# Cross-attention over 64 sequences: weights loaded in whole chunks, and two biases spread on the chip

## The chip, the cores and the metric

The kernel runs on one core of one Trainium2 chip. The metric is the device time of one execution in microseconds. Before the change the median of three runs is 1337.42 us (1336.81 to 1337.81).

## The reference

Everything is fp32. For each of 64 batch entries there are 256 text rows x of width 512 and 256 audio rows c of width 384. The constants of the shapes are B = 64, L = S = 256, H = 512.

```python
text_p = einsum('bld,dh->blh', x, W_text) + b_text
audio_p = einsum('bsd,dh->bsh', c, W_audio) + b_audio
Q = layer_norm(text_p, g1, beta1)
K = layer_norm(audio_p, g2, beta2)
alpha = softmax(einsum('blh,bsh->bls', Q, K) / sqrt(512))
H_hyper = einsum('bls,bsh->blh', alpha, audio_p)
H_hyper = einsum('blh,hk->blk', H_hyper, W_out) + b_out
out = layer_norm(H_hyper + x, g_out, beta_out)
```

## The kernel before, in words

The five engines are TensorE (PE), VectorE (DVE), ScalarE (ACT), GpSimd (POOL) and SyncE (SP). The whole program is one list of calls in the file. Each call (`k[0].multiply(0, [0])`, `q2.six()`) issues one or a few instructions on its engine, and each engine works through its own in the order of the list; semaphores hold an instruction until its inputs are there. So the list is the schedule. It has an opening, a loop over the batch entries 3 to 60 in which five entries are in work at different stages, and an ending. The products of the loop are split by recursive schemes with fewer multiplies (`Fork` for the queries, `Thirds` for the keys and for the output), whose sums of operands stand on DVE and POOL.

The opening is where the change is. Batch entry 0 has no transposed input yet: `RowTurn` takes its rows (c_0, x_0), puts their columns in the kernel's order on DVE (`arrange`), transposes them on PE (tile ps_rows) and copies them to SBUF on ACT (cT, xT). `Projection.multiply(t, chunks)` then multiplies 128 rows by chunks of 128 rows of the weight, 512 wide, into a PSUM bank: ps_m and ps_l for the keys of entry 0, ps_u and ps_n for its queries, ps_f for the keys of entry 1. `evict` adds the bias, so it needs the bias in all 128 partitions. `means` and `centre` take the mean of each weight row and of the bias away. `turn_weights` transposes w_audio (ps_wa), and `fold_multiply` multiplies it by w_out. At the very start `keep_busy(6)` lets PE multiply a tile of ones that nobody reads.

Rows of a weight are dealt to partitions so that partition 32q + i of chunk k holds row 32(qK + k) + i, with q from 0 to 3 and K chunks (3 for w_audio, 4 for w_text). In DRAM a chunk is therefore four separate blocks of 32 rows of 2 KB.

SP issues nearly all DMA requests, in its own order. Eight semaphores are used in turn, so a request also waits until the one eight places before it has landed; ACT issues two requests at the start. `squares` loads an entry in four requests of 32 partitions.

Of the kernel before, what the change touches and what calls it, by code (L numbers as in the profile page):

```python
# [22 lines left out]
def kernel(  # L23
# [87 lines left out]
    nc.gpsimd.memset(ones, 1.0)  # L111
# [16 lines left out]

    x_0 = xin.tile([P, LT, D], F32, tag="x", name="x_0")
# [59 lines left out]
    class RowTurn:  # L189
# [6 lines left out]

        def tile(self, t):
            ar = self.ar[:, t]
            arrange(ar, self.rows[:, t, :], self.chunks, nc.vector.tensor_copy)
            ps = p_at.tile([P, self.chunks, P], F32, tag="at", name="ps_rows")  # L200
            for j in range(self.chunks):
                nc.tensor.transpose(ps[:, j, :], ar[:, j, :], ident)
            nc.scalar.copy(self.T[:, :, bass.ts(t, P)], ps)
# [1195 lines left out]

    keep_busy(6)  # L1400
    war = []
    bt_row = bt_sb.rearrange('p (o h) -> p o h', o=1)
    c_turn = RowTurn(c_0, AC, 'cT')
    var_0 = small.tile([P, 4], F32, tag='var4', name='var')
    wa_t = const.tile([P, 11, WP], F32, tag='wa_thirds', name='wa_thirds')
    wao_room = const.tile([P, HC * H], F32, tag='wo', name='wao_thirds')
    pool, tag = (once, 'e')
    c_turn.tile(0)
    k[0] = Projection('k', 0, c_turn.T, wa_sb, ba_sb, AC, ST, bank[0:2])
    war.append(pool.tile([P, HC, P], F32, tag=tag, name=f'war_{0}'))  # L1410
    x_turn = RowTurn(x_0, DC, 'xT')
    c_turn.tile(1)
    k[0].multiply(0, [0])
    pool, tag = (work, 'eT')
    k[0].multiply(1, [0])
    arrange(war[0], wa_sb[:, 0, :], HC, nc.gpsimd.tensor_copy)
    q[0] = Projection('q', 0, x_turn.T, wt_sb, bt_sb, DC, LT, bank[2:4])
    war.append(pool.tile([P, HC, P], F32, tag=tag, name=f'war_{1}'))
    arrange(war[1], wa_sb[:, 1, :], HC, nc.gpsimd.tensor_copy)
    k[0].multiply(1, [1])  # L1420
    mean_wa = means(wa_sb, AC, 'mwa')
    pool, tag = (work, 'eT')
    war.append(pool.tile([P, HC, P], F32, tag=tag, name=f'war_{2}'))
    k[0].multiply(0, [1])
    k[0].multiply(1, [2])
    arrange(war[2], wa_sb[:, 2, :], HC, nc.gpsimd.tensor_copy)
    x_turn.tile(0)
    ba_row = ba_sb.rearrange('p (o h) -> p o h', o=1)
    x_turn.tile(1)
    k[0].multiply(0, [2])  # L1430
    turn_weights(0, 1)
    q[0].multiply(1, [0])
    q[0].multiply(1, [1])
    centre(wa_sb, mean_wa, AC)
    mean_wt = means(wt_sb, DC, 'mwt')
    mean_ba = means(ba_row, 1, 'mba')
    q[0].multiply(0, [0])
    k[0].evict(1)
    k[0].evict(0)
    third_weights(wa_sb, wa_t, [0])  # L1440
    k[0].scales()
    k[0].normalise([1])
    q[0].multiply(0, [1])
    bt_step = const.tile([P, H2], F32, tag='bt_step', name='bt_step')
    mean_bt = means(bt_row, 1, 'mbt')
    cT[1] = turn_c(1)
    k[0].normalise([0])
    q[0].multiply(0, [2])
    q[0].multiply(0, [3])
    turn_weights(1, 1)  # L1450
    turn_weights(2, 1)
    k[1] = Projection('k', 1, cT.pop(1), wa_sb, ba_sb, AC, ST, bank[4:6])
    q[0].multiply(1, [2])
    k[1].multiply(1, [0])
    centre(ba_row, mean_ba, 1)
    k[1].multiply(0, [0])
    turn_weights(3, 1)
    k[1].multiply(1, [1])
    third_weights(wa_sb, wa_t, [2], nc.vector)
    xT[1] = turn_x(1)  # L1460
    q[0].multiply(1, [3])
    k[1].multiply(1, [2])
    k[1].multiply(0, [1])
    k[1].multiply(0, [2])
    fold_multiply(1, 0, 1)
    xs_1 = SumX(xT.pop(1), nc.vector)
    centre(wt_sb, mean_wt, DC)
    centre(bt_row, mean_bt, 1)
    q[0].evict(1)
    g1_sb, be1_sb, g2_sb, be2_sb, bac_sb = take_columns()  # L1470
    wa_blocks = third_weights(wa_sb, wa_t, [3])
    q[0].evict(0)
    wt_blocks = weight_sums(wt_sb, DC // 2, 'wtsum')
    fold_multiply(1, 1, 2)
    k[0].store()
    xs_1.add(1)
    xs_1.add(1)
    load_c(2)
    folds.append(p_at.tile([P, H], F32, tag='at', name='ps_fold'))
    xs[1] = xs_1  # L1480
    k[1].evict(1)
    q[1] = Fork(1, xs.pop(1).of, wt_blocks)
    load_x(2)
    k[1].evict(0)
    xs_1.add(1)
    fold_multiply(1, 2, 3)
    q[0].scales()
    fold_multiply(0, 0, 1)
    third_weights(wa_sb, wa_t, [1], nc.vector)
    part = bias_parts()  # L1490
    load_c(3)
    cT[2] = turn_c(2)
    Fork.seed()
    cs[2] = Sides(cT.pop(2), 'csum')
    q[0].normalise([0])
    cs[2].add(1)
    fold_multiply(2, 0, 1)
    q[1].seven()
    cs[2].add(1)
    cs[2].add(1)  # L1500
    q[1].one()
    nc.vector.tensor_tensor(bt_step, bt_sb[:, :H2], bt_sb[:, H2:], ALU.subtract)
    nc.vector.tensor_scalar(g2_sb, g2_sb, scale, None, ALU.mult)
    q[1].after_seven()
    xT[2] = turn_x(2)
    k[0].fetch()
    q[0].normalise([1])
    nc.vector.tensor_scalar(be2_sb, be2_sb, scale, None, ALU.mult)
    xs[2] = SumX(xT.pop(2))
    xs_1.add(1)  # L1510
    q[0].store()
    fold_multiply(0, 1, 2)
    fold_multiply(0, 2, 3)
    q[1].after_one()
    k[1].square()
    k[1].scales()
    q[1].six()
    q[1].start_q3()
    fold_multiply(0, 3, 4)
    q[1].step_r()  # L1520
    fold_evict(0)
    cs[2].add(1)
    cs[2].add(1)
    cs[2].add(1)
    load_x(3)
    Thirds.seed_with(ba_sb)
    cT[3] = turn_c(3)
    xs[2].add(1)
    cs[2].add(1)
    load_c(4)  # L1530
    bias_rest(part, 1, 2)
    fold_multiply(1, 3, 4)
    xs[2].add(1)
    ba_delta = third_bias(ba_sb, 'ba_delta')
    cs[3] = Sides(cT.pop(3), 'csum')
    k2_0 = k[2] = Thirds('k', 2, cs.pop(2), wa_blocks, ba_sb, ba_delta)
    q[0].fetch()
    q[1].five()
    k2_0.one()
    fold_evict(1)  # L1540
    q[1].after_five()
    xs[2].add(1)
    at_0 = att[0] = Attention(0)
    xs[2].add(1)
    cs[3].add(1)
    k2_0.copy_n1()
    q[2] = Fork(2, xs.pop(2).of, wt_blocks)
    k[1].normalise([0])
    k2_0.two()
    k[1].normalise([1])  # L1550
    at_0.k.turn()
    cs[3].add(1)
    q[1].two()
    third_weights(wa_sb, wa_t, [4], nc.vector)
    q[1].three()
    k2_0.start_t()
    cs[3].add(1)
    q[1].four()
    xT[3] = turn_x(3)
    q[1].square()  # L1560
    k[1].store()
    q[1].scales()
    fold_multiply(2, 1, 2)
    k2_0.three()
    k2_0.copy_t()
    var_2 = small.tile([P, 4], F32, tag='var4', name='var')
    fold_multiply(2, 2, 3)
    q2_0 = q[2]
    k2_0.start_l0()
    k2_0.start_l1()  # L1570
    cs[3].add(1)
    q[1].normalise([0])
    q[1].normalise([1])
    bias_rest(part, 2, 3)
    fold_multiply(2, 3, 4)
    q[1].store()
    cs[3].add(1)
    k2_0.four()
    Fork.seed()
    xs[3] = SumX(xT.pop(3))  # L1580
    cs[3].add(1)
    at_0.affine_keys(0)
    q2_0.one()
    k2_0.take_m()
    bias_rest(part, 3, 4)
    k2_0.start_u()
    q2_0.seven()
    q2_0.after_one()
    xs[3].add(1)
    fold_evict(2)  # L1590
    at_0.affine_keys(3)
    at_0.q.turn()
    load_c_rows(1)
    q2_0.six()
    q2_0.after_seven()
    q2_0.start_q3()
    load_x(4)
    k2_0.five()
    at_0.affine_queries(3)
    xs[3].add(1)  # L1600
    at_0.affine_queries(0)
    q[1].fetch()
    cs[3].add(1)
    k2_1 = k[3] = Thirds('k', 3, cs.pop(3), wa_blocks, ba_sb, ba_delta)
    last_1 = att[0]
    xs[3].add(1)
    k2_0.copy_n()
    k2_0.copy_u()
    xs[3].add(1)
    q[3] = Fork(3, xs.pop(3).of, wt_blocks)  # L1610
    q2_0.step_r()
    q2_0.five()
    k2_0.leave_middle()
    wao_t = wao_room[:, :11 * WP].rearrange('p (n h) -> p n h', n=11)
    at_0.affine_keys(2)
    at_0.affine_keys(1)
    k2_0.middle_d()
    k2_0.leave()
    q2_0.after_five()
    q2_1 = q[3]  # L1620
    fold_bias(part)
    k2_0.square(var_0[:, 2:], [0])
    at_0.score(0, 1)
    k2_0.leave_ends()
    at_0.affine_queries(2)
    q2_0.three()
    at_0.affine_queries(1)
    k2_0.middle_sum()
    k2_0.square(var_0[:, 2:], [1])
    third_weights(wao_sb, wao_t, [1])  # L1630
    q2_0.two()
    k2_0.seed()
    k[1].fetch()
    q2_0.four()
    at_0.score(1, 2)
    load_c(5)
# [289 lines left out]
    for b in range(3, B - 3):  # L1926
# [32 lines left out]
        if b + 4 < B: load_c(b + 4)  # L1959
# [516 lines left out]
```

## Time and profile before

| what | value |
| --- | --- |
| median of three runs | 1337.42 us |
| the profiled execution's own time | 1338.2 us |
| its span, first to last instruction | 1336.0 us |
| granted TensorE clock | 1.000 |
| instructions | 29959 |
| mean traffic of the DMA engines | 241 GB/s |

The profiled execution's own time includes 2.2 us that lie outside the span. In the rows that follow, a line such as `13.23 1.72 PE ps_n L440 x4` of the chain of waits means that from 13.23 us on, for 1.72 us, four records of PE that write the tile ps_n from line 440 were what the end waited for. An fp32 multiply leaves two records. The matmul rows' ends are modelled, and a few records can be missing. The DMA rows give the requests by tile, their size, and the median time from the issue to the landing where the profile can tell it.

### The profile page before, as it was taken

What the parts mean: (1) busy time and instruction counts of PE and PEld (TensorE: products, weight loads), DVE (VectorE), ACT (ScalarE), POOL (GpSimd) and SP (SyncE); (2) the same over time, 40 slices, a digit from 0 to 9 for tenths busy, and PEclk for the clock granted to TensorE, in tenths of its full rate; (3) what the DMA queues carried; (4) which work ended last, traced back from release to release, by engine and by line L of the source; (5) the groups of instructions that cost most, each with busy time, mean ns of one, the idle gap of its engine ahead of it and who ended that gap; (6) DMA issues with size and microseconds to landing.
All of it is one profiled execution on the core that took longest, in us unless ns stands there. A gap on an engine that the chain in (4) does not pass through costs nothing.

```text
span 1336.0 us, 29959 instructions
## 1 busy us (share of the span) xinstructions
PE 1328.3 (99%) x8495; PEld 1249.6 (94%) x8495; DVE 1243.0 (93%) x3313; ACT 1162.9 (87%) x3310; POOL 1151.5 (86%) x1855
## 2 busy tenths in 40 slices
PE   9999999999999999999999999999999999999998
PEld 5899999999999999999999999999999999999996
DVE  6769999999999999999999999999999999999968
ACT  4898898898898898988988988988889889889885
POOL 5798898898898898988988988988989889889865
PEclk9999999999999999999999999999999999999999
DMA  9988989888888889889888898889988998888773
GB/s 220 243 235 236 242 246 246 242 255 240 251 251 247 245 247 240 259 244 238 255 234 242 253 243 247 243 230 266 254 235 251 255 240 252 246 244 253 209 229 138
DMA packets 448971, 322.24 MB, mean 241 GB/s; under 512 B 153765, under 2 KB 381349, under 8 KB 448806
## 3 DMA queue, kind: packets, MB, share of 16 engines
q1 hardware_dynamic: 448710, 320.20, 85.8%
q8 instruction: 68, 1.11, 0.4%
q14 instruction: 97, 0.79, 0.2%
q10 hardware_dynamic: 96, 0.13, 0.0%
HBM read 203.57 MB, written 116.65 MB: 240 GB/s over the span
## 4 chain that ended last, share of the span: by engine, by line
PE 98%; DMA 1%; ACT 1%; SPq 0%; DVE 0%; issue 0%; DVEq 0%; ACTq 0%
PE ps_f L733 28%; PE ps_m L557 16%; PE ps_sc L884 13%; PE ps_n L557 11%; PE ps_u L557 8%; PE ps_z L1033 7%; PE ps_l L557 5%; PE ps_z L1095 5%; PE ps_sc L823 1%; DMA eq<-ed 1%; PE ps_f L440 0%; PE ps_n L440 0%; PE ps_l L244 0%; PE ps_fold L244 0%; PE ps_u L440 0%; PE ps_m L244 0%
## 5 line engine op out<-in xcount | busy, mean ns | idle before, releaser
L869 POOL TENSOR_TENSOR qsum<-qT 128x256 f32<-128x256 f32 x118 | 112.5, 953 | 101.4 <-ACT qT L527 96.9
L352 POOL TENSOR_TENSOR csum<-csum,cT 128x256 f32<-128x256 f32 x310 | 194.0, 627 | 5.2
L733 PE MATMUL ps_f<-wtsum,xsum 128*128 128x256 f32 x756 | 194.0, 380 | 0.0
L527 ACT ACTIVATE qT<-qT,columns 128x256 f32<-128x256 f32 x256 | 152.2, 597 | 1.8 <-DVE qT L76 1.8
L733 PEld LDWEIGHTS ps_f<-wtsum,xsum 128*128 128x128 f32 x756 | 131.9, 191 | 11.4 <-issue 1.0
L527 ACT ACTIVATE kT<-kT,columns 128x256 f32<-128x256 f32 x256 | 141.2, 609 | 0.0
L733 PE MATMUL ps_f<-wt,xT 128*128 128x256 f32 x504 | 129.5, 379 | 0.0
L884 PE MATMUL ps_sc<-kT,qT 128*128 128x128 f32 x928 | 122.4, 275 | 0.0
L884 PEld LDWEIGHTS ps_sc<-kT,qT 128*128 128x128 f32 x928 | 114.8, 192 | 0.0
L884 PE MATMUL ps_sc<-ksum,qsum 128*128 128x128 f32 x696 | 106.2, 275 | 0.9 <-DVE ps_sc L541 0.9
L1357 DVE SCALAR_TENSOR_TENSOR yr<-yr,rstd,beo 128x512 f32<-128x512 f32 x120 | 106.6, 889 | 0.1
L884 PEld LDWEIGHTS ps_sc<-ksum,qsum 128*128 128x128 f32 x696 | 97.7, 191 | 5.0 <-DVE ps_sc L541 2.2
L733 PEld LDWEIGHTS ps_f<-wt,xT 128*128 128x128 f32 x504 | 91.0, 191 | 9.7
L1348 DVE SCALAR_TENSOR_TENSOR yr<-yr,nm,go 128x512 f32<-128x512 f32 x124 | 95.9, 774 | 0.0
L488 ACT ACTIVATE kr<-kr,rstd 128x512 f32<-128x512 f32 x126 | 92.7, 738 | 0.0
L314 POOL TENSOR_TENSOR xsum<-xT 128x256 f32<-128x256 f32 x124 | 90.6, 732 | 1.9 <-DVE xT L76 1.9
L541 DVE TENSOR_TENSOR ps_l<-ps_m,t 128x171 f32<-128x171 f32 x248 | 83.5, 337 | 7.8 <-ACT t L605 3.3
L1158 ACT ACTIVATE junk<-yr,nm 128x512 f32<-128x512 f32 x124 | 90.2, 727 | 0.3
L794 ACT ACTIVATE junk<-ps_f 128x512 f32<-128x512 f32 x126 | 75.2, 597 | 15.6 <-PE ps_f L733 13.5
L520 DVE STREAM_TRANSPOSE kT<-kq 128x512 f32<-128x512 f32 x122 | 85.3, 701 | 2.9 <-DMA kq<-kd 2.8
L804 ACT ACTIVATE qr<-ps_f,rstd 128x512 f32<-128x512 f32 x126 | 87.8, 699 | 0.1
L1095 PE MATMUL ps_z<-eT,c 128*128 128x256 f32 x296 | 84.6, 380 | 0.0
(302 smaller groups left out, 4653.7 us busy)
## 6 DMA issues: line engine op xcount, KB each, us to landing
kd<-kr SPq DMA_DIRECT2D x64, 512.0 KB, 2.9
kq<-kd SPq DMA_DIRECT2D x256, 128.0 KB, 3.1
qd<-qr SPq DMA_DIRECT2D x64, 512.0 KB, 2.8
qq<-qd SPq DMA_DIRECT2D x256, 128.0 KB, 2.8
xq<-in_x_dram SPq DMA_DIRECT2D x252, 128.0 KB, 3.1
x<-in_x_dram SPq DMA_DIRECT2D x63, 512.0 KB, 5.3
out_dram<-yr SPq DMA_DIRECT2D x62, 512.0 KB, 5.1
cq<-in_ctx_dram SPq DMA_DIRECT2D x252, 96.0 KB, 4.0
```

Of the source, the lines that this page charges most:

```text
L314: self.engine.tensor_tensor(*step)
L352: nc.gpsimd.tensor_tensor(*step)
L488: nc.scalar.mul(row, row, self.r[t])
L527: nc.scalar.activation(self.T[:, k, :], self.T[:, k, :], AF.Identity, bias=bet[:, k : k + 1], scale=gam[:, k : k + 1],)
L557: nc.tensor.matmul(place, lhsT=self.sides.of[n], rhs=self.weights[n], start=(n == 14), stop=True, skip_group_check=True,)
L733: nc.tensor.matmul(place, lhsT=side, rhs=w, start=(n == 7 and c == 0), stop=True, skip_group_check=True,)
L869: nc.gpsimd.tensor_tensor(*self.steps[n])
L884: nc.tensor.matmul(self.place(t, m), lhsT=self.qsides[n][:, c], rhs=self.ksides[n][:, c], start=False, stop=True, skip_group_check=True,)
L1033: nc.tensor.matmul(self.zp[{1: 0, 2: 0, 4: 2}.get(n, 1)], lhsT=self.asides[n], rhs=self.bsides[n], start=(n == 7), stop=True, skip_group_c ...
L1095: nc.tensor.matmul(ps, lhsT=c_rows[self.b][:, s, bass.ts(j, P)], rhs=self.eT[:, s, :], start=start, stop=(s == ST - 1), skip_group_check=True,
L1348: nc.vector.scalar_tensor_tensor(row, row, self.nm[:, t : t + 1], go_sb, ALU.add, ALU.mult)
L1357: nc.vector.scalar_tensor_tensor(self.y[:, t, :], self.y[:, t, :], self.r[t], beo_sb, ALU.mult, ALU.add)
```

## The change

The tile of ones is set by DVE instead of POOL. A weight chunk (256 KB) is one request instead of parts of four: `weight_chunk` issues seven requests where `weight_chunks` issued fourteen. The two input biases are no longer broadcast from DRAM to 128 partitions (256 KB each). `Spread` loads each as 8 KB into 16 partitions, each 32-wide piece four times over; PE transposes this to 128x16 (ps_spread), ACT copies it out with each value repeated 32 times, and DVE transposes 32x32 blocks, which leaves the whole bias in every partition. `RowTurn` can work on single chunks, and the first rows of c are arranged, transposed and copied in pieces. The list of calls is a new one in the opening, the loop and the ending; the loop's calls are the same, in another order. Cut to its core:

```diff
-    nc.gpsimd.memset(ones, 1.0)
+    nc.vector.memset(ones, 1.0)
...
+    class Spread:
+
+        def __init__(self, dst, v, tag):
+            self.dst = dst
+            room = once.tile([P, 3, 2, P], F32, tag=tag, name="spread").rearrange("p a b c -> p (a b c)")
+            self.part, self.full = room[: H // SQ, H : H + P], room[:, :H]
+            nc.sync.dma_start(
+                self.part.rearrange("k (q i) -> k q i", q=NQ),
+                v.rearrange("(k o i) -> k o i", o=1, i=SQ).broadcast_to([H // SQ, NQ, SQ]),
+            )
+
+        def transpose(self):
+            self.ps = p_at.tile([P, H // SQ, 1], F32, tag="at", name="ps_spread")
+            nc.tensor.transpose(self.ps[:, :, 0], self.part, ident[: H // SQ, : H // SQ])
+
+        def copy(self):
+            nc.scalar.copy(
+                self.full.rearrange("p (k j) -> p k j", j=SQ), self.ps.broadcast_to([P, H // SQ, SQ])
+            )
+
+        def turn(self):
+            nc.vector.transpose(self.dst, self.full)
...
-    def weight_chunks(t, w, lo, n, queues):
-        v = w.rearrange("(q k i) h -> q i k h", q=NQ, i=SQ)
-        for q in range(NQ):
-            queues[q].dma_start(t[q * SQ : (q + 1) * SQ, lo : lo + n], v[q, :, lo : lo + n])
-
-    for t in range(ST):
-        nc.sync.dma_start(c_0[:, t, :], c_first[:, t, :])
-    weight_chunks(wa_sb, w_audio, 0, 1, [nc.scalar, nc.sync, nc.scalar, nc.sync])
-    weight_chunks(wa_sb, w_audio, 1, 2, [nc.sync] * NQ)
+    def weight_chunk(t, w, k, queue=nc.sync):
+        queue.dma_start(t[:, k, :], w.rearrange("(q k i) h -> q i k h", q=NQ, i=SQ)[:, :, k])
+
+    nc.sync.dma_start(c_0[:, 0, :], c_first[:, 0, :])
+    weight_chunk(wa_sb, w_audio, 0, nc.scalar)
+    nc.sync.dma_start(c_0[:, 1, :], c_first[:, 1, :])
+    weight_chunk(wa_sb, w_audio, 1)
+    weight_chunk(wa_sb, w_audio, 2)
     for t in range(LT):
         nc.sync.dma_start(x_0[:, t, :], x_first[:, t, :])
-    weight_chunks(wt_sb, w_text, 0, 2, [nc.sync] * NQ)
-    ba_sb = row(b_audio, "ba")
-    weight_chunks(wt_sb, w_text, 2, 2, [nc.sync] * NQ)
+    for n in range(2):
+        weight_chunk(wt_sb, w_text, n)
+    ba_sb = const.tile([P, H], F32, tag="ba", name="ba")
+    spread_ba = Spread(ba_sb, b_audio, "ksum")
+    for n in range(2, DC):
+        weight_chunk(wt_sb, w_text, n)
     blocks = {}
     load_c(1)
-    bt_sb = row(b_text, "bt")
+    bt_sb = const.tile([P, H], F32, tag="bt", name="bt")
+    spread_bt = Spread(bt_sb, b_text, "qsum")
     load_x(1)
...
+        def arrange(self, t, lo, n):
...
+        def transpose(self, t, lo, n):
+            self.ps[t, lo] = p_at.tile([P, n, P], F32, tag="at", name="ps_rows")
+            for j in range(n):
+                nc.tensor.transpose(self.ps[t, lo][:, j, :], self.ar[:, t, lo + j, :], ident)
+
+        def copy(self, t, lo, n):
+            nc.scalar.copy(self.T[:, lo : lo + n, bass.ts(t, P)], self.ps[t, lo])
```

The requests at the head of SP's order, before the change. A row gives the tile, its source, the shape of the SBUF side and how many follow each other; wa and wt are the two input weights, cq and xq the squares of entry 1, wo the output weight:

```order
L142 DMA c_107<-in_ctx_dram 128x384 x2
L139 DMA wa<-in_L_xattn_W_audio_dram 32x512 x2
L139 DMA wa<-in_L_xattn_W_audio_dram 32x2x512 x4
L146 DMA x_106<-in_x_dram 128x512 x2
L139 DMA wt<-in_L_xattn_W_text_dram 32x2x512 x4
L123 DMA ba<-in_L_xattn_b_audio_dram 128x512
L139 DMA wt<-in_L_xattn_W_text_dram 32x2x512 x4
L73 DMA cq_132<-in_ctx_dram 32x8x96 x4
L123 DMA bt<-in_L_xattn_b_text_dram 128x512
L73 DMA xq_139<-in_x_dram 32x8x128 x4
```

And with the change:

```order
L162 DMA c_107<-in_ctx_dram 128x384
L164 DMA c_107<-in_ctx_dram 128x384
L160 DMA wa<-in_L_xattn_W_audio_dram 128x1x512 x2
L168 DMA x_106<-in_x_dram 128x512 x2
L160 DMA wt<-in_L_xattn_W_text_dram 128x1x512 x2
L135 DMA spread<-in_L_xattn_b_audio_dram 16x4x32
L160 DMA wt<-in_L_xattn_W_text_dram 128x1x512 x2
L73 DMA cq_124<-in_ctx_dram 32x8x96 x4
L135 DMA spread<-in_L_xattn_b_text_dram 16x4x32
L73 DMA xq_132<-in_x_dram 32x8x128 x4
```

The sequence of the tensors is the same; the weights' requests went from 32 partitions to 128, one chunk each, and the biases from 128x512 to 16x4x32. ACT issues the first chunk of wa, before two of its four parts.

On PE, in the opening, from the turn of x_0 (ps_rows) to the multiplies of entry 0's queries (ps_n, ps_u), before the change:

```order
L202 MATMUL ps_rows<-ident,xTr 128x128 x8
L440 MATMUL ps_m<-wa,cT_167 128x512
L215 MATMUL ps_wa<-ident,war_179 128x128
L215 MATMUL ps_wa<-ident,war_193 128x128
L215 MATMUL ps_wa<-ident,war_203 128x128
L440 MATMUL ps_n<-wt,xT_181 128x512 x2
L440 MATMUL ps_u<-wt,xT_181 128x512 x4
```

And with the change, from the last multiply of entry 0's keys:

```order
L480 MATMUL ps_l<-wa,cT_154 128x512
L142 MATMUL ps_spread<-ident,spread 128x16
L480 MATMUL ps_u<-wt,xT_185 128x512
L255 MATMUL ps_wa<-ident,war_162 128x128
L255 MATMUL ps_wa<-ident,war_167 128x128
L255 MATMUL ps_wa<-ident,war_187 128x128
L480 MATMUL ps_n<-wt,xT_185 128x512 x3
L480 MATMUL ps_u<-wt,xT_185 128x512
L142 MATMUL ps_spread<-ident,spread 128x16
L480 MATMUL ps_u<-wt,xT_185 128x512
L480 MATMUL ps_n<-wt,xT_185 128x512
L480 MATMUL ps_u<-wt,xT_185 128x512
```

The two transposes of the biases now stand on PE between the multiplies: that of b_audio ahead of the first multiply by wt, that of b_text after the fifth, with three multiplies behind it.

More of the change, by code (lines that the diff above doesn't have):

```diff
@@ L1536 @@
[L1536 to L1555, printed above, removed]
@@ L1622 @@
[L1622 to L1636, printed above, removed]
-    at_0.score(2, 3)
-    q2_0.square(var_0[:, :2], [0])
-    at_0.score(3, 4)
-    cT[4] = turn_c(4)
+    q[1].square()
+    fold_multiply(2, 3, 4)
@@ new lines @@
+    k[1].store()
+    q[2] = Fork(2, xs.pop(2).of, wt_blocks)
+    k2_0.three()
+    q[1].scales()
+    cs[3].add(1)
+    third_weights(wa_sb, wa_t, [2], nc.vector)
+    last_1 = att[0]
+    old_2 = att[0]
+    q2_0 = q[2]
+    q[1].normalise([1])
+    q[1].normalise([0])
+    k2_0.two()
+    Fork.seed()
+    q2_0.seven()
+    at_0.k.turn()
+    xT[3] = turn_x(3)
+    k2_0.copy_t()
+    load_x(4)
+    q2_0.one()
+    k2_0.start_l0()
+    q2_0.after_one()
+    at_0.affine_keys(3)
+    q2_0.after_seven()
@@ L1641 @@
+    q2_0.three()
+    q2_0.two()
+    q2_0.four()
+    xs[3].add(1)
+    xs[3].add(1)
+    k2_1.copy_n1()
+    k2_1.start_t()
+    k2_0.square(var_0[:, 2:], [0])
+    k2_0.seed()
+    bias_rest(part, 2, 3)
+    q2_0.square(var_0[:, :2], [0])
+    at_0.score(1, 2)
+    k2_0.square(var_0[:, 2:], [1])
+    at_0.score(2, 3)
+    at_0.score(3, 4)
+    bias_rest(part, 3, 4)
+    q[3] = Fork(3, xs.pop(3).of, wt_blocks)
     q2_0.square(var_0[:, :2], [1])
-    var_1 = small.tile([P, 4], F32, tag='var4', name='var')
@@ L1823 @@
-    k2_2.middle_d()
     q2_2.two()
     q2_2.three()
+    q2_2.four()
+    k2_2.square(var_2[:, 2:], [0])
+    beo_sb = row(beta_out, 'beo')
+    old_2.o.copy_n1()
+    last_2.open_context()
+    at_2.score(1, 2)
+    old_2.zsides.add(1)
+    old_2.o.start_t()
+    cs[5].add(1)
+    last_2.c_step(0)
+    q[3].turn()
+    q2_2.square(var_2[:, :2], [0])
+    at_2.affine_keys(3)
+    old_2.o.three()
+    k2_2.middle_sum()
+    old_2.o.two()
+    old_2.zsides.add(1)
+    at_2.score(2, 3)
+    xs[5].add(1)
@@ new lines @@
+    k2_m3.leave()
+    att[B - 2].affine_queries(0)
+    old_m3.zsides.add(1)
+    at = att[B - 2]
+    k2_m3.leave_ends()
+    add_bias(B - 2, [0])
+    at_m3.leave_22()
+    old_m3.o.seed()
+    q2_m3.three()
+    q2_m3.four()
+    k2_m3.square(var_m3[:, 2:], [0])
+    old_m3.o.copy_n1()
+    done.store()
+    k2_m3.middle_sum()
+    at_m3.score_block(2)
+    old_m3.o.start_t()
+    k2_m3.square(var_m3[:, 2:], [1])
+    q2_m3.square(var_m3[:, :2], [0])
+    at_m3.query_step(3)
+    old_m3.o.three()
@@ L2277 @@
+    old.o.three()
     settled.totals()
[L2278 to L2298 removed]
@@ L2335 @@
+    at.copy_one()
+    old.o.last_01(x_rows[B - 4])
+    last.o.one()
+    old.o.last_00()
+    end.k.turn()
+    last.o.copy_n1()
+    settled.last_deviation()
+    old.totals()
+    at.copy_two()
     at.multiply(0, bank[5])
     end.affine_keys(1)
-    last.zsides.add(1)
     end.affine_keys(0)
+    last.o.two()
+    end.affine_keys(2)
+    end.affine_keys(3)
+    last.o.start_t()
+    last.o.three()
+    last.o.copy_t()
+    settled.shift(1)
+    settled.settle(1)
     end.score(0, 1)
-    old.o.last_01(x_rows[B - 4])
```

1537 lines of the change are left out of this document (752 added, 785 removed).

## The prediction

> **What bounds the kernel now.** I read the page's busy table first, then the chain of work that ended last, because a share of busy time alone does not say who waits.
>
> ```profile
> PE 1328.3 (99%) x8495; PEld 1249.6 (94%) x8495; DVE 1243.0 (93%) x3313; ACT 1162.9 (87%) x3310; POOL 1151.5 (86%) x1855
> PE 98%; DMA 1%; ACT 1%; SPq 0%; DVE 0%; issue 0%; DVEq 0%; ACTq 0%
> ```
>
> TensorE (PE) is both the busiest engine and 98% of the chain, so the end moves by exactly what PE loses or gains. Next, the loop. Two equal places of neighbouring iterations in the chain, early and late, and the stretches in the middle:
>
> ```profile
> 103.16 1.73 PE ps_f L733 x8
> ...
> 123.45 1.73 PE ps_f L733 x8
> ...
> 1241.22 1.73 PE ps_f L733 x8
> 1261.52 1.73 PE ps_f L733 x8
> ```
>
> ```profile
> 0.00:10.00 10.00, 8.38 (x26) 5.59 (x27) 1.92 (x5) 4.31 (x9) 3.34 (x13) 1.00 0.75 213
> 10.00:20.00 10.00, 10.00 (x37) 5.33 (x36) 7.33 (x16) 6.35 (x16) 5.77 (x12) 1.00 1.13 234
> ...
> 200.00:600.00 400.00, 400.00 (x2647) 383.93 (x2647) 385.98 (x1039) 356.20 (x1027) 356.23 (x571) 1.00 0.89 247
> 600.00:1000.00 400.00, 399.08 (x2627) 381.84 (x2627) 384.22 (x1047) 354.92 (x1019) 354.79 (x569) 1.00 0.88 245
> ```
>
> An iteration takes 20.29 to 20.30 us and PE never stops in it, but for 0.92 us in one place between 600 and 1000. (The columns are span, then PE, PEld, DVE, ACT and POOL busy, the granted clock, the DMA share and GB/s.) The loop has nothing to give; what the change can move lies in the opening. Its chain, column one the start, column two the time:
>
> ```profile
> 0.72 3.19 DMA c<-in_ctx_dram
> ...
> 3.94 0.56 DVE cTr L179
> ...
> 4.54 1.63 PE ps_rows L202 x6
> 6.18 1.56 PE ps_m L440 x2
> 7.74 1.72 PE ps_l L440 x4
> ...
> 11.17 0.87 PE ps_rows L202 x8
> 12.05 0.86 PE ps_m L440 x2
> 12.91 0.33 PE ps_wa L215 x3
> 13.23 1.72 PE ps_n L440 x4
> 14.95 3.43 PE ps_u L440 x8
> ```
>
> One request, the first 128 rows of c, is waited for; from 4.54 on PE is fed without a hole. A 512-wide multiply is two records, 0.86 us; three transposes of the square weight are 0.33.
>
> **The change part by part.** TensorE's work stays: every multiply of before is there, two 16-wide transposes are added. ScalarE gets two copies of 128x512 more (0.54 us each, by the two xT copies below) and VectorE two transposes of 128x512 (0.70 us, by the kT row); behind each the bias is ready 1.2 us after it lands.
>
> ```profile
> 11.65 1.07 ACT L203 COPY xT<-ps_rows 128x512 f32<-128x512 f32 x2 [2.08 <-PE ps_rows L202]
> L520 DVE STREAM_TRANSPOSE kT<-kq 128x512 f32<-128x512 f32 x122 | 85.3, 701 | 2.9 <-DMA kq<-kd 2.8
> ```
>
> I cost these four at nothing: their first readers are evictions and row means, and between bt's transpose and the next multiply into the banks those evictions free stand sixteen 512-wide multiplies, 13.8 us of PE rows. Without that cover they would cost 1.2 us per bias.
>
> The part that decides is the shape of the weight requests. Before, w_audio and w_text come in 14 requests of 32 partitions each; now in seven, each of 128 partitions on the SBUF side, and on the DRAM side four separate blocks of 32 rows. How many of the 16 DMA engines take part in a request can be counted in this trace, because each engine that takes part ends it with a small packet of its own:
>
> ```profile
> DMA packets 448971, 322.24 MB, mean 241 GB/s; under 512 B 153765, under 2 KB 381349, under 8 KB 448806
> ...
> q10 hardware_dynamic: 96, 0.13, 0.0%
> ...
> kd<-kr SPq DMA_DIRECT2D x64, 512.0 KB, 2.9
> ...
> cq<-in_ctx_dram SPq DMA_DIRECT2D x252, 96.0 KB, 4.0
> ...
> eq<-ed SPq DMA_DIRECT2D x244, 64.0 KB, 4.9
> ...
> vectors<-in_L_xattn_g_dram SPq DMA_DIRECT2D x2, 2.0 KB
> vectors<-in_L_xattn_beta_dram SPq DMA_DIRECT2D x2, 2.0 KB
> bo<-in_L_xattn_b_out_dram SPq DMA_DIRECT2D x1, 2.0 KB
> vectors<-in_L_xattn_b_audio_dram SPq DMA_DIRECT2D x1, 2.0 KB
> ```
>
> Queue q10 is ScalarE's and holds just two requests of 32 rows of 2 KB: 64 rows and 32 end packets, so 16 engines each. The same over the whole program: data packets under 512 bytes are those of cq (256 a request, 96 floats each), of eq (256, 64 floats) and of vectors (16, 32 floats): 64512 + 62464 + 80 = 127056. That leaves 153765 - 127056 = 26709 end packets for the 1674 requests of this list (28 rows, kd to vectors). Sixteen each would be 26784; 75 are missing, and 75 is 5 x 12 + 15: the five vectors requests, whose outermost dimension is 4, ended on 4 engines, and bo's single row on one. So the outermost dimension sets the number of engines. The new weight requests have 128 outermost on one side and 4 on the other, which no request of before has. An engine has to take whole outermost pieces of both sides, so I take 4 engines; 16 is the other bound. The Trainium skill states it so: "DMA: Bandwidth & Descriptors", section "Why a DMA increments its semaphore by 16 and not by 1", has the number as the largest one up to 16 that divides the slowest dimension of both access patterns, and always the lowest-numbered engines. By that rule it is 4 and the same 4 for all seven requests, and the sum is the one below; by a split of the SBUF side alone it is 16, and the sum that of the first rival. The count above agrees with the rule where both sides are 4.
>
> On four engines a 256 KB chunk is 64 KB or 32 rows of 2 KB for each. The time of a row, from q10 in a stretch with room on the engines, and from the full queue:
>
> ```profile
> q10 hardware_dynamic: 96, 0.13, 13.0%
> ```
>
> ```profile
> DMA packets 268, 0.45 MB, mean 224 GB/s; under 512 B 49, under 2 KB 49, under 8 KB 268
> ...
> q1 hardware_dynamic: 268, 0.45, 103.3%
> ```
>
> The first is the window 2 to 5 us: 13.0% of 16 x 3 us is 6.24 us for 64 rows and 32 end packets, at most 0.0975 us a row. The second is 9 to 11 us: 33.1 us for 219 rows, 0.151. I take 0.09, since the other twelve engines will be nearly idle and the end packets take a little of the 6.24. (The same page's section "Specifications" has about 27 GiB/s for an engine: as an estimate 0.071 us a row, and 1340.9 us in the sum below; the row measured here decides.)
>
> Now the queue as the order of SP shows it. On the four engines stand, ahead of the request for b_text: c 16 rows of 1.5 KB (worth 12), three wa chunks 96, x 16, four wt chunks 128, cq's four requests 24 KB (12): 264 rows x 0.09 = 23.8 us. First bytes move at 1.7 us, by the zeros of the GB/s row of the window 0 to 3.5 us (0.0875 us a slice, 19 empty):
>
> ```profile
> GB/s 0 0 0 0 0 0 0 0 0 0 0 0 0 0 0 0 0 0 0 18 35 105 53 53 88 298 339 263 363 351 381 351 427 410 392 386 415 281 299 293
> ```
>
> From the last byte to the landing I take 0.7 us (the c request above, 3.19 us in all, leaves at most 2.2 after its first byte). So bt lands at 1.7 + 23.8 + 0.7 = 26.2. PE, in order, reaches bt's transpose when it has done what before had done at 13.23, and three weight transposes and five multiplies more: 13.23 + 0.33 + 5 x 0.86 = 17.9. It waits 8.3 us. The earlier waits (wa's chunks, b_audio, wt's first three chunks) all end before 26.2 and add nothing to it. The last wt chunk alone would be 252 rows and land at 25.1, wanted at 17.9 + 0.86: 6.3 us, the lower figure if bt were not in the way. Behind it the next input that PE needs is wo, after 6.7 us of PE rows; xq and wo are 48 rows more, 4.3 us at 0.09 and 7.2 at 0.151, so at most half a microsecond, and I add nothing.
>
> After such a pause PE's first records are slow: in the opening above the first multiply took 1.56 us for two records, 0.86 later, though the granted clock reads 1.00 throughout. I take 0.3 us (bounds 0 and 0.7). The Trainium skill, "TensorE: Matmul & The Clock Gate", Part 1, has half rate for about 3.4 us after an idle window of that length, up to 1.7 us lost; with it the sum would be 1347.4.
>
> The pieces of c, the earlier `ones` and the moves of the opening are swallowed by the wait: 0 (alone, see the first rival). The new order in the loop has the same 67 PE instructions per iteration: 0. The tail stores the last half rows the other way round: 0, within half a microsecond.
>
> Sum: 8.3 + 0.3 = 8.6 us. The profiled span goes from 1336.0 to 1344.6; its own time is 1338.2, 2.2 above its span, and 0.8 above the median of the three runs. On the median: 1337.4 + 8.6 = 1346.0. Bounds, with four engines: 0.08 us a row (were an end packet to cost near half a row) and wt deciding gives 1.7 + 20.2 + 0.7 - 18.8 = 3.8, so 1341; 0.0975 and the slow records gives 28.1 - 17.9 + 0.7 = 10.9, so 1348.3; with a part of the queue at the crowded figure about 1350.
>
> **The rivals.** *Sixteen engines after all.* The requests might be split by the SBUF side's 128. Then the seven requests are at least as good as the 14, two broadcasts of 256 KB shrink to 8 KB, and no wait is added. PE could start c's first transpose after a 128-wide copy instead of the 0.56 us one, and the first multiply is bounded by wa's chunk 0:
>
> ```profile
> 5.67 0.61 POOL L179 COPY war<-wa 128x512 f32<-128x512 f32 x1 [3.70 <-DMA wa<-in_L_xattn_W_audio_dram]
> ```
>
> The chunk is there at 5.67 at the latest, the multiply stands at 6.18: 0.5 us earlier, 1336.9, bounds -1.2 to +1. For it: 128 is a dimension that before's requests also split by. Against it: four blocks cannot be dealt to 16 engines without cutting them. This is the case that is not slower.
>
> *A wait in the loop.* VectorE works 385.98 of 400 us there, 0.7 us to spare in an iteration, and its rows stand in a new order. If one PE wait of 0.1 us came in each of the loop's 58 iterations (3 to 60), with 16 engines, it is 5.8 us: 1342.7. It decides from 0.05 us an iteration. For it: the small room. Against it: PE's own rows move by no more than two or three places in the iteration, and the room was enough before with the same instructions.
>
> *Everything at once in its favour.* Sixteen engines, the single wait near 668 us gone, and a shorter tail:
>
> ```profile
> 667.71 7.22 DMA eq<-ed
> ```
>
> 0.5 + 0.9 + at most 1.3 is 2.7: 1334.7, only just a gain that can be told.
>
> **How the numbers follow.** Four engines 0.76 (0.72 of it within 1341 to 1350), sixteen with no new wait 0.18, a loop that waits 0.03, all in its favour 0.03. The likeliest is 1346.0, its own range 1341 to 1350. To leave out no more than 2 in 10 the range has to reach into the second case, so it goes down to 1336.5. About 0.2% (2.7 us) is what a measurement of this kernel can tell from no change: faster 0.03, same 0.18, slower 0.79 (a four-engine outcome that hides below 2.7 us is in no row that I see).
>
> **What would show it.** Right: in the opening the profile has PE idle for several microseconds before ps_spread and the wt multiplies, the wt requests land near 16, 19, 22 and 25 us, the DMA share of the first 25 us falls far below before's 0.75 to 1.13, and from the loop on every place stands some 8 us later with a period of 20.30. Wrong: wt's last chunk lands before 17 us; or the shares stay near 1; or the loop's period is longer, whatever the opening does. If PE waits for wt rather than for bt, the mechanism holds and the place of bt in the queue was misjudged.

## The result and the profile after

The changed kernel takes 1348.76 us (median of five runs, 1346.39 to 1351.08) against 1337.42 before (1336.81 to 1337.81): a ratio of 1.0084, 95% interval 1.0072 to 1.0095, so 11.3 us slower. The profiled execution is the shortest of the five, 1346.39 us with a span of 1344.6 and a granted clock of 0.999. The profiles therefore have 8.6 us between them (1336.0 to 1344.6), the medians 11.3; both numbers are explained below.

The page after, busy times and the chain that ended last:

```profile
PE 1332.3 (99%) x8497; PEld 1248.6 (93%) x8497; DVE 1259.1 (94%) x3318; ACT 1175.2 (87%) x3313; POOL 1172.0 (87%) x1854
...
PE 97%; DMA 1%; SPq 1%; DVE 0%; issue 0%; DVEq 0%
```

PE is still what the end waits for, with a little more DMA and SP in the chain than before. Where, the chain of the opening shows (start, time, what):

```profile
1.63 8.48 DMA wa<-in_L_xattn_W_audio_dram
...
10.90 2.53 SPq L160
...
13.47 2.55 SPq L73
...
16.57 2.53 SPq L73
...
20.57 7.05 DMA spread<-in_L_xattn_b_text_dram
27.62 0.14 issue
27.76 0.21 PE ps_spread L142
27.97 1.05 PE ps_u L480 x2
```

Before, the chain of the opening was PE from 4.54 us on. Now it is one transfer, SP's issues and another transfer up to 27.62 us, and PE only from there. What PE waited for on the way stands in brackets in its timeline (the idle time before the row, and what ended it):

```profile
7.82 2.04 PE L480 MATMUL ps_m<-wa,cT 128*128 128x512 f32 x2 [3.21 <-DMA wa<-in_L_xattn_W_audio_dram]
...
20.02 0.20 PE L142 MATMUL ps_spread<-ident,spread 16*128 16x16 f32 x1 [2.25 <-DMA spread<-in_L_xattn_b_audio_dram]
...
22.17 3.70 PE L480 MATMUL ps_n<-wt,xT 128*128 128x512 f32 x6
...
27.76 0.21 PE L142 MATMUL ps_spread<-ident,spread 16*128 16x16 f32 x1 [1.03 <-DMA spread<-in_L_xattn_b_text_dram]
```

There are three waits, each for an input that comes with the whole-chunk requests or behind them, and slow records between them: the six records of ps_n take 3.70 us here and 2.74 in experiments 1 and 4. The DMA side by stretches, in the columns of the prediction (DMA share and GB/s at the end), and the loop:

```profile
0.00:10.00 10.00, 5.75 (x19) 4.24 (x20) 1.35 (x6) 1.92 (x3) 1.83 (x10) 1.00 0.48 139
10.00:20.00 10.00, 7.77 (x24) 3.72 (x23) 0.85 (x2) 4.15 (x10) 1.23 (x2) 1.00 0.33 112
20.00:30.00 10.00, 8.95 (x20) 4.22 (x21) 5.86 (x12) 4.95 (x13) 0.00 (x0) 0.83 0.60 160
...
200.00:600.00 400.00, 400.00 (x2645) 382.81 (x2644) 390.74 (x1049) 360.31 (x1022) 363.55 (x573) 1.00 0.88 247
600.00:1000.00 400.00, 400.00 (x2644) 382.71 (x2643) 390.49 (x1045) 360.87 (x1028) 364.11 (x572) 1.00 0.88 248
```

Between 10 and 20 us the DMA engines are a third busy, 1.13 before. The 0.83 in the row from 20 to 30 us is the granted clock: in slices of 0.2 us it reads 0.50 from 20.7 to 24.1 us, where the slow records of ps_n stand, and 1.00 on both sides. In the loop PE never stops, and the wait of 0.9 us near 675 us that the kernel before had is gone. How many engines a chunk runs on can be counted as in the prediction, since ScalarE's queue, q10, now holds one request alone, chunk 0 of w_audio. Its row on the page:

```profile
q10 hardware_dynamic: 132, 0.26, 0.1%
```

128 rows of 2 KB leave 4 end packets of the 132. The request ran on four engines.

### The profile page after: what moved, and what is told of

Same layout as the page of the kernel before. It is cut to its first block, busy times and chain, and to the rows that moved or that the text cites. A ratio compares the mean times of both kernels' runs of the same rounds, so it can differ in the third digit from the quotient of the medians.

```text
span 1344.6 us, 29708 instructions
## 1 busy us (share of the span) xinstructions
PE 1332.3 (99%) x8497; PEld 1248.6 (93%) x8497; DVE 1259.1 (94%) x3318; ACT 1175.2 (87%) x3313; POOL 1172.0 (87%) x1854
## 4 chain that ended last, share of the span: by engine, by line
PE 97%; DMA 1%; SPq 1%; DVE 0%; issue 0%; DVEq 0%
PE ps_f L773 28%; PE ps_m L597 16%; PE ps_sc L924 13%; PE ps_n L597 11%; PE ps_u L597 8%; PE ps_z L1073 7%; PE ps_l L597 5%; PE ps_z L1135 5%; PE ps_sc L863 1%; DMA wa<-in_L_xattn_W_audio_dram 1%; DMA spread<-in_L_xattn_b_text_dram 1%; SPq L73 1%; PE ps_f L480 0%; PE ps_fold L284 0%; PE ps_m L284 0%; PE ps_l L284 0%
## 5 line engine op out<-in xcount | busy, mean ns | idle before, releaser
L392 POOL TENSOR_TENSOR csum<-csum,cT 128x256 f32<-128x256 f32 x310 | 201.7, 651 | 0.7
L909 POOL TENSOR_TENSOR qsum<-qT 128x256 f32<-128x256 f32 x118 | 85.9, 728 | 59.2 <-ACT qT L567 58.7
L567 ACT ACTIVATE kT<-kT,columns 128x256 f32<-128x256 f32 x256 | 133.9, 594 | 0.7 <-DVE kT L76 0.7
L924 PE MATMUL ps_sc<-kT,qT 128*128 128x128 f32 x928 | 131.8, 275 | 0.0
L1397 DVE SCALAR_TENSOR_TENSOR yr<-yr,rstd,beo 128x512 f32<-128x512 f32 x120 | 122.7, 1023 | 0.1
L924 PEld LDWEIGHTS ps_sc<-kT,qT 128*128 128x128 f32 x928 | 121.3, 192 | 0.0
L1388 DVE SCALAR_TENSOR_TENSOR yr<-yr,nm,go 128x512 f32<-128x512 f32 x124 | 109.4, 883 | 0.0
L528 ACT ACTIVATE kr<-kr,rstd 128x512 f32<-128x512 f32 x126 | 85.0, 728 | 0.0
L500 ACT ACTIVATE junk<-kr 128x512 f32<-128x512 f32 x126 | 80.8, 641 | 0.3
L844 ACT ACTIVATE qr<-ps_f,rstd 128x512 f32<-128x512 f32 x126 | 79.9, 689 | 0.1
```

What stands on the lines that cost most here:

```text
L392: nc.gpsimd.tensor_tensor(*step)
L567: nc.scalar.activation(self.T[:, k, :], self.T[:, k, :], AF.Identity, bias=bet[:, k : k + 1], scale=gam[:, k : k + 1],)
L909: nc.gpsimd.tensor_tensor(*self.steps[n])
L924: nc.tensor.matmul(self.place(t, m), lhsT=self.qsides[n][:, c], rhs=self.ksides[n][:, c], start=False, stop=True, skip_group_check=True,)
L1388: nc.vector.scalar_tensor_tensor(row, row, self.nm[:, t : t + 1], go_sb, ALU.add, ALU.mult)
L1397: nc.vector.scalar_tensor_tensor(self.y[:, t, :], self.y[:, t, :], self.r[t], beo_sb, ALU.mult, ALU.add)
```

## The experiments

Each kernel is compared with the kernel before, run beside it on the same chip (1337.3 to 1337.7 us there).

**1. The requests undone.** The change, with the weights asked in 14 requests of 32 partitions as before:

```diff
-    def weight_chunk(t, w, k, queue=nc.sync):
-        queue.dma_start(t[:, k, :], w.rearrange("(q k i) h -> q i k h", q=NQ, i=SQ)[:, :, k])
+    def weight_chunks(t, w, lo, n, queues):
+        v = w.rearrange("(q k i) h -> q i k h", q=NQ, i=SQ)
+        for q in range(NQ):
+            queues[q].dma_start(t[q * SQ : (q + 1) * SQ, lo : lo + n], v[q, :, lo : lo + n])
```

> The changed kernel, with the weights asked for as before the change (14 requests of 32 partitions); the pieces, the spread biases and the new order stay. If the four-block requests cost the time, all wait goes: 1336.9 us, from 1336.2 to 1338.4, and b_text's 8 KB are on the chip before TensorE's place for them, about 17.9 us. If it is the biases' new path (request, transpose, copy, transpose) or the new order, the time stays above 1345.

1338.47 us (1337.64 to 1340.34), ratio 1.0007, 0.9998 to 1.0016: just above the top of the expected range. The chain of the opening and the page's q10 row:

```profile
2.11 3.28 DMA wa<-in_L_xattn_W_audio_dram
5.38 0.25 issue
5.63 2.05 PE ps_m L479 x2
...
19.62 0.16 PE ps_spread L142
19.79 1.06 PE ps_u L479 x2
```

```profile
q10 hardware_dynamic: 96, 0.13, 0.0%
```

96 packets are again 64 rows and 32 end packets, sixteen engines for each of the two requests. The three waits are gone but for 0.4 us of the first; from 5.63 us on PE has no hole in the opening, and b_text's transpose stands at 19.62 instead of 27.76, 8.1 us earlier. The spans differ by 8.0 (1344.6 and 1336.6). So the shape of the weight requests costs what is lost, and the rest of the change together (spread biases, pieces, new order) makes no difference that can be measured.

**2. Fewer engines still.** The change, with each chunk asked in two requests of two blocks (64 partitions) each:

```diff
-        queue.dma_start(t[:, k, :], w.rearrange("(q k i) h -> q i k h", q=NQ, i=SQ)[:, :, k])
+        v = w.rearrange("(q k i) h -> q i k h", q=NQ, i=SQ)[:, :, k]
+        for j in range(2):
+            queue.dma_start(t[64 * j : 64 * j + 64, k, :], v[2 * j : 2 * j + 2])
```

> The changed kernel, with each 256 KB chunk in two requests of two 32-row blocks (64 partitions each). If a request is dealt to as many engines as it has blocks in DRAM, each now runs on two engines, and always the same two: 488 rows at the 0.094 us that the changed kernel's trace gives, b_text lands at about 48 us instead of 27.6, and the run takes about 1367 to 1370 us. If the SBUF side decides (64 partitions, 16 engines) or the plain count of requests does, it is no slower than the changed kernel, at most 1349, and 1337 if all 16 engines work.

1369.15 us in a single run, granted clock 0.990, within the first theory's range. The traffic from 4 to 24 us in 40 slices, of the change and then of this kernel:

```profile
GB/s 91 124 156 320 303 238 135 90 98 98 102 111 98 98 98 102 98 94 102 90 98 102 98 98 98 168 201 172 82 100 96 151 168 90 173 155 95 113 242 112
```

```profile
GB/s 29 43 50 53 49 49 53 53 49 49 49 53 49 49 53 102 217 279 320 197 41 45 49 49 53 49 49 49 49 49 49 49 49 53 49 49 45 49 49 53
```

A plateau of 98 GB/s with four blocks in DRAM, of 49 with two: 24.5 GB/s a block. The packets of q10 say the same: 132 here too, now for two requests of 64 rows, which leaves two end packets for each. With twice the requests and half the bytes in each, the traffic halves, while experiment 1, with as many requests of the same sizes, moves a mean of 213 GB/s in the same 20 us. So it is neither the number of requests nor their size, nor the SBUF side's number of partitions (128, 64, and 32 there); the outermost dimension on the DRAM side sets how many engines work. The rule that the prediction took from the Trainium skill ("DMA: Bandwidth & Descriptors", "Why a DMA increments its semaphore by 16 and not by 1") also holds where the two sides differ, 128 against 4 and 64 against 2.

**3. The requests alone.** The kernel before, with nothing changed but that its weights are asked in seven whole chunks:

```diff
-    weight_chunks(wt_sb, w_text, 0, 2, [nc.sync] * NQ)
+    weight_chunk(wt_sb, w_text, 0)
+    weight_chunk(wt_sb, w_text, 1)
```

(and the same for the other chunks).

> The kernel before, with nothing changed but the seven whole-chunk requests (biases broadcast from DRAM as before, old order). If the four-block requests are the cause: w_text's chunks 2 and 3 land near 23.5 and 26.5 us, wanted at 16.7 and 17.5, a wait of about 9 us: 1346.5 us, from 1344 to 1350. If the new order or the spread biases are needed for the loss: 1337.4, within 1 us.

1350.61 us (1350.00 to 1352.43), ratio 1.0098, 1.0084 to 1.0112: the requests alone cost 13.0 us, more than the whole change.

```profile
1.63 8.86 DMA wa<-in_L_xattn_W_audio_dram
...
12.26 15.59 DMA wt<-in_L_xattn_W_text_dram
27.85 0.04 issue
27.89 1.13 PE ps_u L441 x2
```

Here w_text's last chunk ends the stall, 27.85, though no spread bias exists: the expectation's cause was right and its size 4 us low, outside its range. The two profiled spans (1336.0 and 1348.2) are 12.2 us apart. 10.4 of it is the wait: the multiply that needs this chunk starts at 27.89 instead of 17.53 (14.95 in the chain before, and three multiplies of 0.86 us). Most of the rest is slow records behind it: the granted clock reads 0.50 from 29.3 to 32.7 us, and 3.4 us at half rate lose 1.7. Experiments 1 and 3 together: the requests explain the whole loss, and the rest of the change takes back perhaps 2 us of it (1348.76 and 1350.61; the two ratios' intervals overlap, and 2 us is little more than one such slow stretch).

**4. PE kept busy while it waits.** The change, with 14, 10 and 6 multiplies of ones ahead of the three waits:

```diff
+    keep_busy(14)
     k[0].multiply(0, [0])
...
+    keep_busy(10)
     spread_ba.transpose()
...
+    keep_busy(6)
     spread_bt.transpose()
```

> The changed kernel, with TensorE multiplying the tile of ones 14, 10 and 6 times more ahead of its three waits in the opening (w_audio's first chunk, b_audio, b_text); nobody reads these products. The waits stay, so the profiled time stays near 1346. If the spread of the changed kernel's runs (1346.4 to 1351.1) is TensorE's clock coming back late after the waits, the median falls from 1348.8 to about 1346.5 and the runs lie within 1 us of each other; if the spread comes from the transfers, the median stays near 1348.8 with the same spread.

1347.10 us (1346.50 to 1347.13), ratio 1.0068, 1.0056 to 1.0081. The waits stay:

```profile
22.06 2.74 PE L480 MATMUL ps_n<-wt,xT 128*128 128x512 f32 x6
...
28.42 0.20 PE L142 MATMUL ps_spread<-ident,spread 16*128 16x16 f32 x1 [1.43 <-DMA spread<-in_L_xattn_b_text_dram]
```

But the records between them are short (ps_n 2.74 instead of 3.70), and five runs lie within 0.6 us instead of 4.7. So most of what the medians have beyond the profiles, 1.7 of the 2.7 us, and most of the spread of the changed kernel fit PE coming back slowly after its waits, more in some executions than in others. The mean granted clocks on record agree: 0.999, 0.998, 0.995, 0.999 and 0.997 in the five runs of the change, 0.999 or 1.000 here. They do not give the whole spread, since the longest run, 1351.08 us, has 0.998 and one of 1350.07 has 0.995. The intervals of the two ratios overlap, so the 1.7 is less sure than the narrowing.

**5. The biases at the front.** The change, with the two bias requests right behind the first request for w_audio:

```diff
     weight_chunk(wa_sb, w_audio, 0, nc.scalar)
+    spread_ba = Spread(ba_sb, b_audio, "ksum")
+    spread_bt = Spread(bt_sb, b_text, "qsum")
     nc.sync.dma_start(c_0[:, 1, :], c_first[:, 1, :])
```

> The change with nothing moved but the two requests for the biases, which stand right behind the first request for w_audio instead of behind w_text's second chunk and behind the squares of c. If the four engines' queue is what is late and the bias request merely stood at its end: the wait for b_text is gone, w_text's last chunk, which landed at 26.1 us, ends the stall instead, wanted at 18.8: 7.3 us instead of 9.9, so 1346.2 (1345 to 1347.5). If the spread request itself is what is slow (its 64 pieces of 128 bytes, its 16 partitions), its wait moves with it to the front and the time stays at 1348 or grows.

1348.55 us (1347.56 to 1351.72), ratio 1.0084, 1.0069 to 1.0098: no better. The wait for b_text is gone, PE transposes it at 25.84 us instead of 27.76, as the first theory had it; and the time is as the rival had it. PE's timeline shows what took its place:

```profile
25.84 0.23 PE L142 MATMUL ps_spread<-ident,spread 16*128 16x16 f32 x1
...
35.03 1.10 PE L284 MATMUL ps_l<-wo,waT 128*128 128x512 f32 x2 [1.72 <-DVE wt L319]
```

The bracket names DVE, which ended a piece of work at just that time. But this row multiplies by w_out (wo), and its wait is for several semaphores: those of the four wo requests, and one of DVE for the bank, which the eviction of ps_l had set free at 29.8; its operands, wo and waT, do not come from the centring of w_text that the bracket names. So it was most probably another, the last wo request. SP's timeline, and the view of the line that issues wo:

```profile
21.04 6.26 SPq L73 DMA_DIRECT2D xq<-in_x_dram  x4
27.36 1.86 SPq L118 DMA_DIRECT2D wo<-in_L_xattn_W_out_dram  x4
```

```profile
L118 SPq DMA_DIRECT2D wo<-in_L_xattn_W_out_dram x4: 429/431/437, 27.4 to 28.8; - x4
...
DMA to landing us min/median/max: 5.9/6.0/6.2
```

28.8 and 6.0 to 6.2 is 34.8 to 35.0, and PE goes on at 35.03. SP comes to wo that late for two reasons. A request waits for the one eight places before it, and those are w_text's chunks on their four engines: in this trace SP waits 2.4 us for them ahead of the last squares of x. And its issues are slow: the four squares of c take it 6.92 us, 2.47 before the change. In the changed kernel SP reaches wo at 26.97, and PE its first fold at 34.83, with hardly any room. Moving the biases thus took away one of two waits of nearly the same size: the other goes by w_text's chunks, SP and wo. The run does not separate the two cleanly, because the moved requests seem to hold SP back too. In the profile SP's first request for w_text starts at 6.27 us, 4.14 in the change, behind a wait of 1.3 us that ends with b_audio's landing, and the chain of the opening begins with b_text's request, which takes 5.28 us. So the second theory has a part in it: these 8 KB take some 5 us at the front as well.

**6. The biases broadcast.** As in 1, and the biases loaded to 128 partitions from DRAM as before:

```diff
-    spread_ba = Spread(ba_sb, b_audio, "ksum")
+    ba_sb = row(b_audio, "ba")
...
-    spread_bt = Spread(bt_sb, b_text, "qsum")
+    bt_sb = row(b_text, "bt")
```

> The change with its weights asked in 14 requests of 32 partitions as before, and the biases broadcast from DRAM to 128 partitions as before; pieces and new order stay. If spreading the biases on the chip is worth nothing here, as the sum has it: the time of the kernel with spread biases, 1338.5, less two transposes of 0.15 to 0.23 us, 1338.1 (1337.4 to 1339). If the 512 KB of broadcasts crowd the weights out: w_text's chunks land up to 1.2 us later and PE waits for one, 1339 to 1340.

1339.23 us (1338.17 to 1341.79), ratio 1.0016, 1.0007 to 1.0025. What PE waited for between 20 and 60 us (total, times, longest), of this kernel, and from 40 us to the end of experiment 1:

```profile
PE ps_m L594 <- DVE ps_l L578: 1.0, 1, 1.0
PE ps_l L281 <- DVE bt L316: 0.8, 1, 0.8
PE ps_f L770 <- DVE ps_f L578: 0.6, 2, 0.4
```

```profile
PE ps_m L596 <- DVE ps_l L580: 0.3, 1, 0.3
```

The time is in the second theory's range, and by its kind of cause, though not at w_text. The second row stands ahead of the first fold again, in a place where PE needs wo: SP waits 1.4 us for the broadcast of b_audio and 0.5 for that of b_text, issues its last wo request at 18.6 instead of 16.6 in experiment 1, and with 7.1 us to its landing it is there at 25.7; PE goes on at 25.95, while the work of DVE that the row names ended at 25.4. The other rows are DVE's lateness behind the squares. The profiled execution took 1340.91 us, well above the median, so these waits need not be in every run. Against experiment 1 the spread is worth 0.8 us in the medians, with intervals that overlap.

**7. The opening's gaps and pieces.** In experiment 1 PE's records are twice as long until about 9.5 us, and there are two short gaps between them. Three kernels change that, all from experiment 1. The first fills the gaps:

```diff
-    keep_busy(6)
+    keep_busy(8)
...
     c_turn.transpose(0, 1, 2)
+    keep_busy(1)
```

> The change with its weights asked in 14 requests of 32 partitions as before, and two more multiplies of ones at the very start and one ahead of the wait for w_audio's chunk 0, which fill the two gaps of 0.4 to 0.7 us that PE had there. If PE's slow start (its records doubled until about 9.5 us instead of 7) comes from these gaps: PE's records are short from about 6 us, 2 to 2.6 us come back, 1336.2 (1335.5 to 1337.5), ahead of the kernel before or level with it. If the slow start comes from anything else (the load of the engines, the time since the program began): 1338.5 or a little more.

The second handles c's first 128 rows whole:

```diff
-    c_turn.arrange(0, 0, 1)
-    c_turn.arrange(0, 1, 1)
-    c_turn.arrange(0, 2, 1)
+    c_turn.arrange(0, 0, 3)
```

(and so its transposes and its copies).

> The change with its weights asked in 14 requests of 32 partitions as before, and the first 128 rows of c arranged, transposed and copied whole as before instead of in two pieces; the spread biases and the new order stay. If the pieces themselves are worth something: PE's first transpose starts 0.2 us later (the copy is 0.56 us instead of 0.35), and the time is 1338.7 (1338 to 1339.5). If the pieces break PE's start into short bursts with gaps, and so hold its clock back: two gaps become one, PE's records are short before 8 us, and the time is 1337.3 (1336.5 to 1338).

The third is the second with one more multiply of ones at the start:

> The kernel of e8_c_whole with one multiply of ones more at the start (0.49 us, up to 4.46), which fills PE's gap ahead of its first transpose. If gaps hold the clock back: PE's records are short from about 6 us, as before the change, and with its ones half a microsecond earlier the time is 1336.9 (1336 to 1337.5), level with the kernel before or just ahead. If the start of the opening makes no difference to the end, because later waits take up what is gained: 1338.4, as with the gaps filled in the other way.

Measured: 1338.38 (1337.83 to 1339.01), 1338.57 (1337.41 to 1338.96) and 1338.90 us (1337.43 to 1339.40); ratios 1.0005 (0.9997 to 1.0014), 1.0004 (0.9995 to 1.0013) and 1.0007 (0.9998 to 1.0016). All are the time of experiment 1, so the theory that the gaps cost time missed in all three, and the pieces are worth nothing that can be measured. PE's first multiply, in the second kernel and in the third:

```profile
5.81 1.12 PE L479 MATMUL ps_m<-wa,cT 128*128 128x512 f32 x2 [0.57 <-ACT cT L237]
```

```profile
6.17 2.07 PE L479 MATMUL ps_m<-wa,cT 128*128 128x512 f32 x2 [0.57 <-ACT cT L237]
```

The same gap of 0.57 us ahead of it, and once it is short and once long. When PE comes to full rate does not follow from gaps of this size. Nor does the end follow from it. In the first two kernels PE's records were short from the first multiply on (1.06 and 1.12 us), as the theory of the gaps had it, and both profiles were 1.0 us ahead of experiment 1 at 76 us. The first still ended with the same span, 1336.6: the same row of the chain was 0.5 us ahead at 1285, and the rest went in the ending. The second was 0.3 us behind at 1286. The traces name no single wait for it. No version here beats the kernel before.

## Why the prediction was right

*Four engines.* The step that decided was right, by the end packets of q10 (4 beside 128 rows), by the plateaus of 98 and 49 GB/s, and by the run with the requests undone, which came out where the rival of sixteen engines had no new wait to add. (The list that the prediction counts has 29 rows, not 28; its 1674 requests are right.)

*The queue.* 264 rows at 0.09 us were to bring b_text in at 26.2 us; it landed at 27.62. That is 25.2 us of rows instead of 23.8, or 0.0955 us a row: near my upper bound of 0.0975. The last chunks of w_text were to land near 22 and 25. The row means on ACT, which wait for them, began here:

```profile
22.89 0.63 ACT L312 ACTIVATE junk<-wt 128x512 f32<-128x512 f32 x1 [0.67 <-DMA wt<-in_L_xattn_W_text_dram]
...
26.18 0.63 ACT L312 ACTIVATE junk<-wt 128x512 f32<-128x512 f32 x1 [2.57 <-DMA wt<-in_L_xattn_W_text_dram]
```

Both are about a microsecond late, 3.29 us apart for 32 rows. A row alone in the plateau takes 0.084 us (2 KB at 24.5 GB/s), so what I mis-sized was probably not the row but what else the four engines had to do, and SP, whose issues I had at no cost; no run takes these apart.

*The wait.* 17.9 was PE's place without a wait, and 27.76 is 9.9 later instead of 8.3: 1.4 from the landing, 0.14 from the issue after it. But the place was itself too early. With the requests undone the same transpose stands at 19.62, because PE's records were slow until about 9.5 us, so the requests cost 8.1 us there and the other 1.7 belong to PE's start. That the earlier waits add nothing held, since all lie ahead of b_text's.

*Nothing behind b_text.* I had wo as the next input that PE needs, late by at most half a microsecond, and added nothing. PE has indeed no wait behind 27.76. But I had wo behind the bytes of the queue and not behind SP: in experiment 5 the way by w_text's chunks, SP and wo puts the fold at 35.0 with no wait for b_text, so the two ways nearly tie, and the stall of this kernel is not b_text's alone.

*The loop, and what was put at nothing.* The period is what I said:

```profile
103.01 0.86 PE ps_f L773 x4
...
123.31 0.86 PE ps_f L773 x4
...
1239.80 0.86 PE ps_f L773 x4
1260.09 0.86 PE ps_f L773 x4
```

20.30 and 20.29 us, although DVE is busier, 390.74 of 400 us instead of 385.98. The rival that waits in the loop is refuted. I had left the wait of 0.9 us near 675 us in the sum; it is gone, which with an ending shorter by 0.3 us gives back 1.2. So it is luck that the sum hit the profiled span of 1344.6 to the tenth. Errors cancel in it: 9.9 less 1.2 where the sum had 8.3 and 0.3.

*The slow records.* The term of 0.3 us is the one that failed for the median. In the profiled execution PE's slow stretches lie ahead of b_text's landing, where they cost nothing, and the first records behind it are nearly full (1.05 us for two). Over the runs it is more: keeping PE busy takes 1.7 us off the median. "TensorE: Matmul & The Clock Gate", Part 1 of the Trainium skill, by which the sum would have been an estimated 1347.4, was nearer to the median of 1348.76. The same part of the Trainium skill has PE's activity watched in a free-running window of 3.4 us, so that the loss depends on where a wait falls in that window. The traces agree: the granted clock is at 0.50 for 3.4 us here (20.7 to 24.1), twice for 3.4 us in experiment 3 (8.8 to 12.2 and 29.3 to 32.7, with starts 20.5 us apart, which is six times 3.4), for 6.8 us in experiment 5 (8.3 to 15.1), and never in experiment 4. On one point they differ, and the measurement decides: the Trainium skill has half rate after an idle window, but in the 3.4 us before the drop at 20.7 PE waited only 2.25 us and worked for the rest. Such a stretch costs 1.7 us when it lies behind the last wait, as in experiment 3, and nothing when it lies ahead of it, as here. What decides in the first microseconds of the program, where the slow records do not show in the granted clock, stays open. Of the last 1.1 us between the kept-busy kernel's median and the sum, 0.7 may be the landing: in its profile b_text's transpose stands at 28.42 instead of 27.76. The rest stays open too.

*Sixteen engines.* The rival's own price, 0.5 us in favour, was wrong by its sign: with the requests undone the change is 0.85 us slower in the medians, within what can be told from no change. PE's first multiply stood at 5.63 instead of 6.18, as that step said, and lost it again to slow records and a wait of 0.3 us for DVE near 48 us.

## What to carry to other kernels

Look at the outermost dimension of both sides of a request before counting requests or bytes: seven large requests with four blocks in DRAM ran at 98 GB/s where fourteen small ones ran at some 213. To size such a delay, list every input behind the slow queue, and every request whose issue waits for one of its landings, since moving one input forward can show the next and hold up others (experiment 5). And a profile that agrees with a forecast to the tenth can still hold two wrong terms; the place-by-place comparison and the run with one part undone tell them apart.

## What the runs showed of the hardware that was not expected

An issue on SP can itself be slow: before the change, two requests for x took 0.90 us together; with four engines behind, single requests took 2.5 us (the rows of SPq in the chain above) and SP reached b_text's request only at 20.57, 13.72 before. No run shows why. And PE's first multiply after the same short gap took 1.12 us in one execution and 2.07 in another while the granted clock of that stretch read 1.00 in both. In the changed kernel, too, the first multiplies take 2.04, 2.00 and 1.91 us for two records up to 14 us, at a granted clock of 1.00, where later ones take 1.02; the drops that come later do show, as 0.50. So that row of the profile is no guide to PE's rate in the first microseconds of a program.
